# Sampling by ramps on row differences, with one four-bank spread tile, in a Trainium2 kernel

## The chip, the core and the metric

The kernel runs on one core of one Trainium2 chip. A core has a matrix engine (TensorE, in the profile PE, with its weight loads as PEld), a vector engine (VectorE, DVE), an activation engine (ScalarE, ACT), a general engine (GpSimd, POOL) and a queue engine (SyncE, SP) that here only issues DMA transfers. Matmuls write to PSUM, which is eight banks of 2 KB for each of 128 partitions; the other engines read it from there and work in SBUF. The engines run side by side, each through its own queue in order, and wait for one another through semaphores. The metric is the time of one execution of the whole kernel on the device, in microseconds (us). Lower is better.

## The reference

The network has four residual layers on an input of 16 images, 32 channels, 128 x 128. The change lies almost wholly in the second half of layer 1, a deformable convolution along y. For each image, each of K = 9 taps and each output place (r, c) an earlier stage gives a real row coordinate y. The tap k reads column c + k - 4 of the input at that row, by linear interpolation between two rows:

```
y0 = jnp.floor(gy)
...
w = (1.0 - jnp.abs(gx - xi)) * (1.0 - jnp.abs(gy - yi))
...
deformed = grid_sample_bilinear(input, grid)
out = conv2d(deformed, dsc_w, dsc_b, stride=(K, 1))
return group_norm(out, gn_w, gn_b, gn_w.shape[0] // 4)
```

The x coordinate is always whole, so only y is interpolated. The nine samples of a place are combined over channels and taps by the weights `dsc_w`; a group norm over groups of four channels follows, and the layer's input is added.

## The kernel before

The layers run one after another: `layer0`, `layer1_offsets`, `layer1_scan`, `layer1_sample`, `layer2`, `layer3_edges`, `layer3_net`. `layer1_sample` is the stage of the change. It has no gather. For one column c, the samples of all 128 places r are a matrix product: the image column as a 128 (rows) x 32 (channels) stationary operand, and a 128 x 128 matrix of hat functions, 1 - |y - row| where that is positive and 0 elsewhere, as the moving one. The stage builds those hats and multiplies.

An image is cut into 32 blocks of four columns; 16 images give 512 blocks. Block m is number n = m mod 32 of its image, and i = n mod 4 is its place in a group of four blocks, for which one convolution is done. For each block there are three kinds of hats:

- `ya`, taps 0 to 3, a 128 x 2048 tile. The y values lie as rows of the tile `Y`. Four matmuls (`spread`, L1212) copy one row of each tap onto all 128 partitions in PSUM, in tiles `pb` of two banks, of which there are two. ScalarE takes each half out as |y - row| (L1213), and VectorE makes the negative hat in place, min(t, 1) - 1 (`hats`, L1217).
- `yd`, taps 4 to 7, a 128 x 2048 tile. Here the DMA itself spreads: `fetch` (L1202) reads 8 KB of y and writes it to all 128 partitions, 1 MB for each block. ScalarE makes |y - row| in place (`absolutes`, L1333), VectorE the hat (L1217).
- `h8`, tap 8, once in four blocks (`eighth`), the same as `ya` from the tile `Y8`.

The sampling itself is `taps` (L1224): 16 matmuls for taps 0 to 3 and 16 for taps 4 to 7, each into a one-bank tile `pd` of which there are two; VectorE copies each to SBUF (`ds`, L1371 and L1377). `last_tap` does tap 8 for four blocks, and ScalarE copies it (L1398). `convolve` (L1259, L1264) multiplies a group's samples with the weights into `po`, ScalarE adds the bias (L1267). `turn` transposes the result through `pt` (L1276), VectorE copies it to `ob` (L1277). `finish` is the group norm of an image, given out in 22 small pieces, one at the end of each block, while the next image is sampled: eight pieces of statistics, two of sums over partitions, twelve of 128 x 1024 elementwise operations (L1320, L1322, L1324), of which each third adds the image `xt` as the residual and stores a quarter of the result.

The order on TensorE, VectorE and ScalarE is the order of the program: a helper, `in_order`, ties each instruction of these engines to the one before it. For block m the program writes: samples of `ya` of block m; `absolutes` and the hats `ya` of block m+1; copy; `near` (the spread of block m+2, with its two ScalarE operations); samples of `yd` of block m; hats `yd` of block m+1; copy. Then comes one of four extras: at i = 0 the convolution of the group before, at i = 1 its transposes, at i = 2 the spread for tap 8, at i = 3 the samples of tap 8. DMA issues on SP are not tied; the framework puts them where it expects their slot to be free. SP works through them in order, so a transfer whose slot is not yet free holds those behind it.

PSUM has eight banks: `pd` two, `po` and `pt` one each, `pb` four.

Of the kernel before, what the change touches and what calls it, by code (L numbers as in the profile page):

```python
# [10 lines left out]
F32 = mybir.dt.float32  # L11
AF = mybir.ActivationFunctionType
# [5 lines left out]
P = 128  # L18
# [50 lines left out]
def layer0(tc, w, x, x1, nb=B):  # L69
# [5 lines left out]
    with ExitStack() as ctx:  # L75
# [200 lines left out]
        def tail_z(st):  # L276
            b, t0 = st["b"], st["t0"]
            pz = ps_1.tile([P, 4, HW], F32, name="pz", tag="pz")
            for k in range(4):
                nc.tensor.matmul(pz[:, k], st["aT"][:, k], wadd, start=True, stop=False)  # L280
                nc.tensor.matmul(pz[:, k], st["mT"][:, k], wmod, start=False, stop=True)
            o = wp.tile([P, 4, HW], F32, name="o", tag="o")
            nc.vector.tensor_add(o, pz, xs[b][:, t0 : t0 + 4])
            r0 = (b % 4) * T + t0
            nc.sync.dma_start(x1[b // 4][r0 : r0 + 4].rearrange("t (c d) -> c t d", d=HW), o)

# [835 lines left out]
def layer1_sample(tc, w, x1, x2, ymap, sb1, batches=range(B)):  # L1122
# [8 lines left out]
    nc = tc.nc  # L1131
    V, S, M = nc.vector, nc.scalar, nc.tensor.matmul
    W4 = 4 * HW
    NB = HW // 4
    batches = list(batches)
    with ExitStack() as ctx:
        cp = ctx.enter_context(tc.tile_pool(name="cc", bufs=1))
        psd = ctx.enter_context(tc.tile_pool(name="cpd", bufs=2, space=PSUM))
        pso = ctx.enter_context(tc.tile_pool(name="cpo", bufs=1, space=PSUM))
        psb = ctx.enter_context(tc.tile_pool(name="cpb", bufs=2, space=PSUM))  # L1140
        dw4 = load(nc, cp, w["dsc_k4"], "dsc_k4")
# [3 lines left out]
        ident = load(nc, cp, w["ident"], "ident")  # L1145
        nrow = load(nc, cp, w["nrow"], "nrow")
        avg = cp.tile([P, P], F32, name="avg", tag="avg")
        V.memset(avg, 1.0 / P)

        sel = cp.tile([P, 32, P], F32, name="sel", tag="sel")  # L1150

        cb = cp.tile([P, NG, 4, 2], F32, name="cb", tag="cb")
        with tc.tile_pool(name="ct", bufs=1) as tp:
            e32 = load(nc, tp, w["eye32"], "eye32")
            V.tensor_copy(sel, e32.unsqueeze(2).to_broadcast([P, 32, P]))
            selq = load(nc, tp, w["selq"], "selq")
            for q in range(4):
                pq = psd.tile([P, NG, 2], F32, name="pq", tag="pd")
                M(pq, selq[:, q], sb1, start=True, stop=True)
                V.tensor_copy(cb[:, :, q], pq)  # L1160
            pb = pso.tile([P, NG, 4], F32, name="pbo", tag="po")
            for n, t in enumerate((dw4[:, 0], dw4[:, 1], dw8)):
                M(pb, t, cb[:, :, :, 1], start=(n == 0), stop=(n == 2))
            bos = cp.tile([P, NG, 4], F32, name="bos", tag="bos")
            V.tensor_scalar_add(bos, pb, bo)
# [12 lines left out]
        def open_image(b):  # L1178
            im = images[b] = {}
            g, j = divmod(b, 4)  # L1180
            im["Y"] = Y = yp.tile([P, W4], F32, name="Y", tag="Y")
            nc.sync.dma_start(Y, ym(b)[0:4].rearrange("k (n f) -> (k n) f", f=W4))
            im["Y8"] = Y8 = yp.tile([P, W4], F32, name="Y8", tag="Y8")
            y8 = ym(b)[8].rearrange("(s q f) -> q s f", q=4, f=W4)
            for q in range(4):
                nc.sync.dma_start(Y8[32 * q : 32 * q + 8], y8[q])
            im["xt"] = xt = xp.tile([P, T, HW], F32, name="xt", tag="xt")
            xg = x1[g][T * j : T * j + T].rearrange("o (r c) -> r o c", c=HW)
            for q in range(4):
                nc.sync.dma_start(xt[:, 8 * q : 8 * q + 8], xg[:, 8 * q : 8 * q + 8])  # L1190

            s = cb[:, g, j, 0:1]
            im["w4"] = w4 = sp.tile([P, 2, T], F32, name="w4", tag="w4")
            V.tensor_scalar(w4, dw4[:, :, 0:T], s, -1.0, ALU.mult, ALU.mult)
            im["w8"] = w8 = sp.tile([P, P], F32, name="w8", tag="w8")
            V.tensor_scalar(w8, dw8, s, -1.0, ALU.mult, ALU.mult)

        def fetch(m):
            b, n = order[m]
            blocks[m] = bl = {}  # L1200
            bl["yd"] = yd = hp.tile([P, 4, W4], F32, name="yd", tag="yd", bufs=4)
            nc.sync.dma_start(  # L1202
                yd, ym(b)[4:8, n * W4 : n * W4 + W4].unsqueeze(0).to_broadcast([P, 4, W4])
            )

        def spread(dst, Y, n, k):

            for h in range(2):
                pb = psb.tile([P, 2, W4], F32, name="pb", tag="pb")
                for a in range(2):  # L1210
                    q = 32 * (2 * h + a)
                    M(pb[:, a], sel[q : q + k, n], Y[q : q + k], start=True, stop=True)  # L1212
                S.activation(dst[:, 2 * h : 2 * h + 2], pb, AF.Abs, bias=nrow)  # L1213

        def hats(t):

            V.tensor_scalar(t, t, 1.0, 1.0, ALU.min, ALU.subtract)  # L1217

# [51 lines left out]
        def turn(b, s, oc):  # L1270

            if s == 0:
                images[b]["ob"] = xp.tile([P, T, HW], F32, name="ob", tag="ob")
            pt = pso.tile([P, 4, P], F32, name="pt", tag="pt")
            for i in range(4):
# [6 lines left out]
        def finish(b):  # L1282

            g, j = divmod(b, 4)
            im = images[b]
            ob, xt = im["ob"], im["xt"]
            st = sp.tile([P, 8, 6], F32, name="st", tag="st")
            mv = sp.tile([P, 8, 2], F32, name="mv", tag="mv")
            for og in range(8):
                V.bn_stats(st[:, og], ob[:, 4 * og : 4 * og + 4])  # L1290
                V.bn_aggr(mv[:, og], st[:, og])
                yield
            pm = pso.tile([P, 4, P], F32, name="pm", tag="pt")[:, 0, 0:8]
            M(pm, avg, mv[:, :, 0], start=True, stop=True)
# [6 lines left out]
            yield  # L1301
            pv = pso.tile([P, 4, P], F32, name="pv", tag="pt")[:, 0, 0:8]
            M(pv, avg, d, start=True, stop=True)
# [10 lines left out]
            for q in range(4):  # L1314
                o = slice(8 * q, 8 * q + 8)
                col = [
                    t.rearrange("p a b -> p (a b)")[:, o].unsqueeze(2).to_broadcast([P, 8, HW])
# [5 lines left out]
                yield  # L1323
                V.tensor_add(ob[:, o], ob[:, o], xt[:, o])  # L1324
                nc.gpsimd.dma_start(  # L1325
# [4 lines left out]

        def absolutes(m):
            yd = blocks[m]["yd"]
            S.activation(yd, yd, AF.Abs, bias=nrow)  # L1333

        def near(m):
            b, n = order[m]
            blocks[m]["ya"] = ya = hp.tile([P, 4, W4], F32, name="ya", tag="ya")
            spread(ya, images[b]["Y"], n, 32)

        def eighth(b, s):  # L1340
            h8 = hp.tile([P, 4, W4], F32, name="h8", tag="h8", bufs=2)
            spread(h8, images[b]["Y8"], s, 8)
            images[b]["h8", s] = h8

        open_image(batches[0])
        NM = len(order)
        for m in range(min(3, NM)):
            fetch(m)
        with in_order(tc, nc.tensor, nc.vector, nc.scalar):
            eighth(batches[0], 0)  # L1350
            near(0)
            absolutes(0)
            near(1)
            hats(images[batches[0]]["h8", 0])
            hats(blocks[0]["ya"])
            hats(blocks[0]["yd"])
            done = iter(())
            for m in range(NM + 6):
                b, n = order[m] if m < NM else (None, m - NM)
                if m < NM:  # L1360
                    bl = blocks[m]
                    bl["ds"] = dp.tile([P, 2, W4], F32, name="ds", tag="ds", bufs=6)
                    if n == 12 and m + NB < NM:
                        open_image(order[m + NB][0])
                    if m + 3 < NM:
                        fetch(m + 3)
                    pd = taps(m, 0, bl["ya"])
                    if m + 1 < NM:
                        absolutes(m + 1)
                        hats(blocks[m + 1]["ya"])  # L1370
                    V.tensor_copy(bl["ds"][:, 0], pd.rearrange("p i r -> p (i r)"))  # L1371
                    if m + 2 < NM:
                        near(m + 2)
                    pd = taps(m, 4, bl["yd"])
                    if m + 1 < NM:
                        hats(blocks[m + 1]["yd"])
                    V.tensor_copy(bl["ds"][:, 1], pd.rearrange("p i r -> p (i r)"))  # L1377
                s, i = divmod(n, 4)
# [16 lines left out]
                elif i == 3 and m < NM:  # L1395
# [4 lines left out]
                    if m + 1 < NM:  # L1400
                        nb_, nn = order[m + 1]
                        hats(images[nb_]["h8", nn // 4])
                next(done, None)
# [954 lines left out]
def network(ctx, tc, w, x, out):  # L2358
# [5 lines left out]

    x1 = [scratch([P, L], f"x1_{g}") for g in range(NG)]
    x2 = [scratch([P, L], f"x2_{g}") for g in range(NG)]
# [36 lines left out]
def pack(inp):  # L2403
# [104 lines left out]
    w["dsc_rows"] = np.tile(np.stack([i["gn_w"], i["gn_b"]])[None], (P, 1, 1))  # L2508
    w["nrow"] = -np.arange(P, dtype=f)[:, None]

# [96 lines left out]
```

## Time and profile before

| what | us |
|---|---|
| median of 3 runs | 16696.99 (16661.64 to 16734.23) |
| the profiled execution | 16668.54 |
| its span | 16666.3 |
| first sampling copy (L1371) to the last | 10778.7 to 13897.0 |
| TensorE busy over the span | 14464.2 |
| VectorE busy | 14412.7 |
| ScalarE busy | 12525.8 |
| GpSimd busy | 9711.4 |

A time in the profile is counted from the start of the span. A row of a group of instructions gives the line, the engine, the operation, what is written and read by the program's names, the shapes, the count, then the busy time in us with the mean of one instruction in ns, and last the idle time of the engine just ahead of them with what ended it. Neighbours on an engine overlap at their edges, so that sums of single durations come out some per cent above the engine's busy time. The clock column (PEclk) is the share of full speed that TensorE was granted; it is either 1 or 0.5 at any moment, so that its mean tells the share of time at half speed.

### The profile page before, as it was taken

To read this page: it belongs to the slowest core of one execution; us is meant where nothing else is said; L and a number is where in the kernel's file an instruction comes from. 1 tells how busy PE (TensorE), PEld (TensorE's weight loads), DVE (VectorE), ACT (ScalarE), POOL (GpSimd) and SP (SyncE) were. 2 spreads that over 40 slices of the span, in tenths; PEclk is the share of its full clock that TensorE was granted. 3 is DMA by queue.
4 is the path that set the end of the run, shared out by engine and by line. 5 is a ranking of instruction groups with operands and counts; after the bars stand their busy time and mean duration, and the time that the engine had idled before them with its cause. 6 is when DMAs were issued, how large, how long until landed. Compare 5 with 4: busy or idle time off the path is not lost. (4 is left out here: it accounts for less than half of the span.)

```text
span 16666.3 us, 327843 instructions
## 1 busy us (share of the span) xinstructions
PE 14464.2 (87%) x126810; PEld 5828.1 (35%) x126810; DVE 14412.7 (86%) x13784; ACT 12525.8 (75%) x25236; POOL 9711.4 (58%) x17789
## 2 busy tenths in 40 slices
PE   8998999989999888888888888899999997689966
PEld 3333333333333432222222222255555554434421
DVE  9999999999999659999999999888888886698622
ACT  8999999999999557777777777598888984466411
POOL 8999999999999457778887888500000001000012
PEclk9999999999999989999999999899899998789977
DMA  0000000000000334444454445578777876444356
GB/s 23 12 13 12 12 18 12 13 13 12 18 12 8 95 110 159 160 161 164 166 166 165 163 165 167 153 186 195 194 201 196 198 194 182 98 83 83 75 150 201
DMA packets 1347602, 1837.19 MB, mean 110 GB/s; under 512 B 161685, under 2 KB 661902, under 8 KB 1335799
## 3 DMA queue, kind: packets, MB, share of 16 engines
q1 hardware_dynamic: 1289910, 1655.23, 36.2%
q0 software_dynamic: 43840, 144.20, 2.4%
q8 instruction: 997, 16.33, 0.4%
q10 hardware_dynamic: 12288, 16.79, 0.4%
q14 instruction: 567, 4.64, 0.1%
HBM read 1497.44 MB, written 229.64 MB: 104 GB/s over the span
## 5 line engine op out<-in xcount | busy, mean ns | idle before, releaser
L235 POOL TENSOR_SCALAR Rp<-su,nv 128x128 f32<-128x128 f32 x15360 | 5406.6, 371 | 167.9 <-PE pS L241 133.0
L239 ACT ACTIVATE Ra<-su,bv 128x128 f32<-128x128 f32 x15360 | 4626.2, 390 | 406.7 <-PE pS L241 403.3
L224 DVE TENSOR_TENSOR Rd<-pu,nv 128x2048 f32<-128x2048 f32 x2176 | 4856.6, 2275 | 17.8 <-PE pS L241 16.8
L241 PE MATMUL pS<-Rd,zw 128*32 128x512 f32 x17408 | 2798.0, 606 | 378.7 <-DVE Rd L224 377.9
L919 DVE TENSOR_TENSOR_SCAN hh<-dd,state,pd 128x512 f32<-128x512 f32 x2304 | 2823.1, 1267 | 152.4 <-ACT ln L834 7.1
L940 POOL TENSOR_TENSOR hh<-hh,bc 128x2048 f32<-128x2048 f32 x512 | 2319.2, 4530 | 450.8 <-DVE state L927 439.8
L1325 POOL DMA_DIRECT2D x<-ob x64 | 92.0, 1438 | 3100.4 <-DVE ob L1324 2766.5
L904 PE MATMUL pd<-du,spread 32*128 32x512 f32 x4608 | 1340.1, 655 | 574.6 <-DVE hh L919 566.7
L896 ACT ACTIVATE dd<-dd,m_a 128x512 f32<-128x512 f32 x2304 | 1514.8, 713 | 335.3 <-DMA dd<-dm 328.9
L914 DVE TENSOR_TENSOR pd<-pd,bc 128x1024 f32<-128x1024 f32 x1152 | 1400.6, 1216 | 58.7 <-ACT bc L877 55.4
L241 PE MATMUL pS<-Rp,zw 128*32 128x512 f32 x7680 | 1314.3, 598 | 26.0 <-POOL Rp L235 25.9
L1333 ACT ACTIVATE yd<-yd,nrow 128x2048 f32<-128x2048 f32 x512 | 1238.1, 2418 | 56.7 <-DMA yd<-ymap 56.7
L1213 ACT ACTIVATE ya<-pb,nrow 128x1024 f32<-128x1024 f32 x1024 | 1196.7, 1260 | 80.6 <-PE pb L1212 80.1
L241 PE MATMUL pS<-Ra,zw 128*32 128x512 f32 x7680 | 1237.3, 601 | 0.0
L1212 PE MATMUL pb<-Y,sel 32*128 32x512 f32 (+1 forms) x5120 | 1075.3, 739 | 176.0 <-ACT ya L1213 172.8
L241 PEld LDWEIGHTS pS<-Rd,zw 128*32 128x32 f32 x17408 | 582.1, 109 | 1484.7 <-DVE Rd L224 927.4
L904 PEld LDWEIGHTS pd<-du,spread 32*128 32x128 f32 x4608 | 371.1, 189 | 1607.4 <-DVE hh L919 726.8
L1217 DVE TENSOR_SCALAR yd<-yd 128x2048 f32<-128x2048 f32 x512 | 727.5, 1421 | 207.0 <-ACT yd L1333 205.8
L1217 DVE TENSOR_SCALAR ya<-ya 128x2048 f32<-128x2048 f32 x512 | 759.0, 1482 | 10.7 <-ACT ya L1213 9.4
L1224 PE MATMUL pd<-ya,xt 128*32 128x128 f32 x16384 | 691.4, 311 | 42.5 <-DVE ds L1377 31.7
L1945 PE MATMUL ps<-t,W 128*128 128x512 f32 x1280 | 635.4, 644 | 80.9 <-DVE W L1925 53.1
L1224 PEld LDWEIGHTS pd<-yd,xt 128*32 128x32 f32 x16384 | 533.2, 178 | 471.0 <-issue 224.7
(434 smaller groups left out, 22927.2 us busy)
## 6 DMA issues: line engine op xcount, KB each, us to landing
dd<-dm SPq DMA_DIRECT2D x2304, 256.0 KB
yd<-ymap SPq DMA_DIRECT2D x512, 1024.0 KB
xq<-x SPq DMA_DIRECT2D x48, 1088.0 KB
dm<-dt POOLq DMA_DIRECT2D x192, 256.0 KB, 3.8
w<-d SPq DMA_DIRECT2D x512, 73.1 KB
xb<-tok SPq DMA_DIRECT2D x248, 144.0 KB
x<-in_x SPq DMA_DIRECT2D x64, 512.0 KB
x<-o SPq DMA_DIRECT2D x128, 256.0 KB
```

What stands on the lines that cost most here:

```text
L224: nc.vector.tensor_tensor(R, st["pu"].unsqueeze(1).to_broadcast([P, 4, 4, HW]), nv[:, :, i::32].rearrange("p t q -> p q t").unsqueeze(3).t ...
L235: nc.gpsimd.tensor_scalar(R[:, q, k], su[:, k], 3.4028234e38, nv[:, k, c], ALU.min, ALU.max)
L239: nc.scalar.activation(R[:, q, k], su[:, k], AF.Relu, bias=bv[:, k, c])
L241: nc.tensor.matmul(st["pS"][32 * q : 32 * q + 32], zw[:, 31 - i : 63 - i], R[:, q], start=first, stop=False, tile_position=(0, 32 * q), sk ...
L896: S.activation(dd[:, r], dd[:, r], AF.Exp, scale=acol[:, dr, d : d + 1])
L904: nc.tensor.matmul(pd[:, a], spread[e, k], st["du"][n][e], start=True, stop=True)
L914: V.tensor_mul(pd, pd, bm.unsqueeze(1).to_broadcast([P, 2, CH]))
L919: V.tensor_tensor_scan(hh[:, r, s], dd[:, r, s], pd[:, a, s], st["state"][:, 4 * i + r : 4 * i + r + 1], ALU.mult, ALU.add,)
L940: G.tensor_mul(hh, hh, st["bc"][1, n].unsqueeze(1).to_broadcast([P, 4, CH]))
L1217: V.tensor_scalar(t, t, 1.0, 1.0, ALU.min, ALU.subtract)
L1224: M(pd[32 * q : 32 * q + 32, i], xt[:, :, xc], h, start=True, stop=True, tile_position=(0, 32 * q),)
L1333: S.activation(yd, yd, AF.Abs, bias=nrow)
```

## The change

The interpolation is rewritten. With D[p] = x[p+1] - x[p], the sample at y is x[0] + sum over p of D[p] * clamp(y - p, 0, 1). The moving operand becomes a ramp, clamp(y - p, 0, 1), in place of a hat, and the stationary one the differences. Row 127 of the operand holds x[0] itself with a ramp that is always 1.

- `layer0` writes row 0 of each channel a second time behind the image (one more DMA of 2 KB for each output tile), and `x1` gets 128 more columns for it.
- `open_image` loads rows 1 to 128 into `xt`. `differ` loads rows 0 to 127 in quarters (`xq`) and GpSimd subtracts them, in blocks 24 to 27 of the image before. `finish` adds `xq`, loaded again by quarters, in place of `xt`. The y rows now lie in three tiles (`Y0`, `Y1`, `Y8`) with a row of ones beside each sixteen, loaded by 19 DMAs instead of 5; the ones and a 17th row of `sel` subtract the row number inside the spread matmul.
- `spread` writes all four matmuls into one `pb` tile of four banks, of which there is one. For `ya`, one VectorE operation takes it out, max 0 then min 1 (`ramp`), in place of two on ScalarE and one on VectorE. For `h8`, one ScalarE operation (Relu) and one VectorE clamp.
- `yd` is made by ScalarE in two halves (`ramps`, Relu with the bias -p), and clamped by VectorE (`clamps`).
- Both copies `ds` move from VectorE to ScalarE; `pd` has three banks instead of two. `pt` and `po` share one bank.
- `yd` has five buffers instead of four and is fetched four blocks ahead instead of three; ScalarE works on block m+2 of `yd` instead of m+1. GpSimd is tied to the program's order too.

```diff
-            nc.sync.dma_start(x1[b // 4][r0 : r0 + 4].rearrange("t (c d) -> c t d", d=HW), o)
+            nc.sync.dma_start(x1[b // 4][r0 : r0 + 4].rearrange("t (c d) -> c t d", d=HW)[0:P], o)
+            nc.sync.dma_start(x1[b // 4][r0 : r0 + 4, L:].unsqueeze(0), o[0:1])
...
-        psd = ctx.enter_context(tc.tile_pool(name="cpd", bufs=2, space=PSUM))
+        psd = ctx.enter_context(tc.tile_pool(name="cpd", bufs=3, space=PSUM))
         pso = ctx.enter_context(tc.tile_pool(name="cpo", bufs=1, space=PSUM))
-        psb = ctx.enter_context(tc.tile_pool(name="cpb", bufs=2, space=PSUM))
+        psb = ctx.enter_context(tc.tile_pool(name="cpb", bufs=1, space=PSUM))
...
+        def quarter(b, q):
+            g, j = divmod(b, 4)
+            xq = xp.tile([P, 8, HW], F32, name="xq", tag="xq")
+            xg = x1[g][T * j + 8 * q : T * j + 8 * q + 8].rearrange("o (r c) -> r o c", c=HW)
+            nc.sync.dma_start(xq, xg[0:P])
+            return xq
+
+        def differ(b, q):
+            xt = images[b]["xt"][0 : P - 1, 8 * q : 8 * q + 8]
+            G.tensor_sub(xt, xt, quarter(b, q)[0 : P - 1])
...
-        def spread(dst, Y, n, k):
-
-            for h in range(2):
-                pb = psb.tile([P, 2, W4], F32, name="pb", tag="pb")
-                for a in range(2):
-                    q = 32 * (2 * h + a)
-                    M(pb[:, a], sel[q : q + k, n], Y[q : q + k], start=True, stop=True)
-                S.activation(dst[:, 2 * h : 2 * h + 2], pb, AF.Abs, bias=nrow)
-
-        def hats(t):
-
-            V.tensor_scalar(t, t, 1.0, 1.0, ALU.min, ALU.subtract)
+        def spread(Y, n):
+
+            pb = psb.tile([P, 4, W4], F32, name="pb", tag="pb")
+            for a in range(4):
+                q = 32 * a
+                M(pb[:, a], sel[q : q + 17, n], Y[q : q + 17], start=True, stop=True)
+            return pb
+
+        def clamps(t):
+
+            V.tensor_scalar_min(t, t, 1.0)
...
+        def ramp(m):
             blocks[m]["ya"] = ya = hp.tile([P, 4, W4], F32, name="ya", tag="ya")
-            spread(ya, images[b]["Y"], n, 32)
+            V.tensor_scalar(ya, blocks[m].pop("pb"), 0.0, 1.0, ALU.max, ALU.min)
+
+        def ramps(m, h):
+            v = blocks[m]["yd"][:, 2 * h : 2 * h + 2]
+            S.activation(v, v, AF.Relu, bias=step)
 
         def eighth(b, s):
             h8 = hp.tile([P, 4, W4], F32, name="h8", tag="h8", bufs=2)
-            spread(h8, images[b]["Y8"], s, 8)
+            S.activation(h8, spread(images[b]["Y8"], s), AF.Relu)
             images[b]["h8", s] = h8
...
-                    if m + 3 < NM:
-                        fetch(m + 3)
-                    pd = taps(m, 0, bl["ya"])
-                    if m + 1 < NM:
-                        absolutes(m + 1)
-                        hats(blocks[m + 1]["ya"])
-                    V.tensor_copy(bl["ds"][:, 0], pd.rearrange("p i r -> p (i r)"))
+                    if 24 <= n < 28 and m + NB < NM:
+                        differ(order[m + NB][0], n - 24)
+                    if m + 4 < NM:
+                        fetch(m + 4)
+                    p0 = taps(m, 0, bl["ya"])
                     if m + 2 < NM:
                         near(m + 2)
-                    pd = taps(m, 4, bl["yd"])
+                    S.copy(bl["ds"][:, 0], p0.rearrange("p i r -> p (i r)"))
+                    if m + 2 < NM:
+                        ramp(m + 2)
+                        ramps(m + 2, 0)
+                    p4 = taps(m, 4, bl["yd"])
+                    S.copy(bl["ds"][:, 1], p4.rearrange("p i r -> p (i r)"))
+                    if m + 2 < NM:
+                        ramps(m + 2, 1)
                     if m + 1 < NM:
-                        hats(blocks[m + 1]["yd"])
-                    V.tensor_copy(bl["ds"][:, 1], pd.rearrange("p i r -> p (i r)"))
+                        clamps(blocks[m + 1]["yd"])
```

## The prediction

> **What bounds the kernel now.** I read the page's slices first (layer 1's sampling is the stretch from 10.74 to 13.9 ms), then the stage's own windows, its instruction groups, TensorE's order of time inside one group of four blocks, and last who waits for transfers. The first sampling copy starts at 10778.7 and the last at 13897.0: 3118.3 us for 511 steps, 6.10 us a block, 24.41 us a group of four. All that follows is counted in such groups, of which there are 128.
>
> The windows of the stage: stretch, its length, then busy time of PE, PEld, DVE, ACT and POOL, granted clock, DMA share, GB/s. The first is a long stretch, the other two are single groups.
>
> ```profile
> 11550.00:12340.00 790.00, 721.73 (x11246) 423.87 (x11240) 686.20 (x733) 702.63 (x519) 23.59 (x16) 0.91 0.80 195
> ...
> 12053.98:12078.24 24.26, 23.06 (x361) 13.25 (x355) 23.23 (x23) 21.37 (x17) 1.72 (x1) 0.86 0.82 199
> 12078.24:12101.71 23.47, 21.21 (x360) 12.49 (x354) 23.47 (x24) 22.60 (x18) 2.71 (x2) 1.00 0.89 232
> ```
>
> Three engines are at 87 to 91%, so no single one can be relieved for much. In the undisturbed group (clock 1.00) VectorE is busy throughout and ScalarE nearly so; the group with a spell at half clock is 0.8 us longer. Its neighbour before it, from 12029.19 to 12053.98, took 24.79 with such a spell too.
>
> The instruction groups that the change touches, and L224 of layer 0 as a row for its new operation:
>
> ```profile
> L224 DVE TENSOR_TENSOR Rd<-pu,nv 128x2048 f32<-128x2048 f32 x2176 | 4856.6, 2275 | 17.8 <-PE pS L241 16.8
> L1333 ACT ACTIVATE yd<-yd,nrow 128x2048 f32<-128x2048 f32 x512 | 1238.1, 2418 | 56.7 <-DMA yd<-ymap 56.7
> L1213 ACT ACTIVATE ya<-pb,nrow 128x1024 f32<-128x1024 f32 x1024 | 1196.7, 1260 | 80.6 <-PE pb L1212 80.1
> L1217 DVE TENSOR_SCALAR ya<-ya 128x2048 f32<-128x2048 f32 x512 | 759.0, 1482 | 10.7 <-ACT ya L1213 9.4
> L1217 DVE TENSOR_SCALAR yd<-yd 128x2048 f32<-128x2048 f32 x512 | 727.5, 1421 | 207.0 <-ACT yd L1333 205.8
> L1371 DVE COPY ds<-pd 128x512 f32<-128x512 f32 x512 | 374.3, 731 | 89.0 <-PE pd L1224 88.0
> L1398 ACT COPY ds<-pd 128x512 f32<-128x512 f32 x128 | 116.5, 910 | 32.9 <-PE pd L1224 32.4
> ```
>
> TensorE in order of time, from a block with i = 2 on:
>
> ```profile
> 12039.15 1.20 PE L1224 MATMUL pd<-yd,xt 128*32 128x128 f32 x32
> 12041.49 2.91 PE L1212 MATMUL pb<-Y,sel 8*128 8x512 f32 x8 [1.13 <-ACT ya L1213]
> 12044.33 2.06 PE L1224 MATMUL pd<-ya,xt 128*32 128x128 f32 x32
> 12046.32 2.09 PE L1212 MATMUL pb<-Y,sel 32*128 32x512 f32 x8
> 12048.34 1.67 PE L1224 MATMUL pd<-yd,xt 128*32 128x128 f32 x32
> 12049.82 1.07 PE L1224 MATMUL pd<-h,xt 128*32 128x128 f32 x32
> 12050.82 1.19 PE L1224 MATMUL pd<-ya,xt 128*32 128x128 f32 x32
> 12051.93 1.14 PE L1212 MATMUL pb<-Y,sel 32*128 32x512 f32 x8
> 12053.01 1.20 PE L1224 MATMUL pd<-yd,xt 128*32 128x128 f32 x32
> 12053.98 1.94 PE L1259 MATMUL po<-ds,w 128*32 128x512 f32 x16
> 12055.85 1.12 PE L1264 MATMUL po<-ds,w 128*128 128x512 f32 x2
> 12056.91 1.20 PE L1224 MATMUL pd<-ya,xt 128*32 128x128 f32 x32
> ```
>
> Start to start at full clock: samples of `ya` 1.11 us, a spread 1.08, samples of `yd` about 1.0, convolution 2.93, samples of tap 8 1.0; the transposes are 0.66. The spread for tap 8 stood 1.13 us for a `pb` tile that ScalarE still held, and after that gap the next bursts took 2.06 and 2.09 in place of 1.2 and 1.14: the matrix engine lost its clock for some 8 us. With a mean clock of 0.91, 18% of the time is at half speed, 4.4 us a group, so about 0.55 such spells a group; one costs now about 1.0 us (24.26 and 24.79 against 23.47).
>
> The waits of the stage for transfers:
>
> ```profile
> ACT yd L1333 <- DMA yd<-ymap: 56.7, 14, 6.8
> ```
>
> Fourteen times in all `yd` was late, 56.7/128 = 0.44 us a group. So 23.47 + 0.55 + 0.44 = 24.46 is the 24.41 measured.
>
> **What the change moves, in sums a group.** ScalarE loses eight `ya` halves (8 x 1.26) and two of tap 8 (2.5), gains eight copies (8 x 0.58 to 0.91; the low end is the 128x512 copy of L877 at 582 ns) and one 128x2048 Relu (2.42 by L1333); four `yd` operations become eight halves (4 x 2.42 to 8 x 1.26). From 24.1 to between 18.4 and 21.6. VectorE loses four hats (4 x 1.48) and eight copies (5.9), gains four ramps. A ramp is new: 128x2048 out of PSUM in one operation. The low end is L224, 2.275, which reads as much from PSUM; the high end four copies `ds`, 4 x 0.731 = 2.92, with four starts. I take 2.5, near the first since it is one instruction, but with the sampling burst always beside it (a `yd` hat is 1.184 at its fastest, 1.421 in the mean). VectorE goes from 23.4 to about 21.6. TensorE's work is the same. By sums alone the change wins about 1.8 us a group.
>
> The row says that PSUM costs VectorE double: a hat of 2048 from SBUF takes 1.184 at best, a copy of 512 from PSUM 0.616. [...]
>
> **What stands on the path.** The sums do not decide, because there is now one `pb`. Each spread must wait until the tile of the one before is read out as a whole. I follow one group at full clock, handoffs at 0.05 (the chain shows 0.03 to 0.04). VectorE's `finish` pieces are 8 x (0.80 + 0.20) + 12 x 1.45 + 1.7 = 27.1 an image, 0.85 a block. Zero is the start of the spread in the block with i = 1.
> - i = 1: spread to 1.08; ramp 1.13 to 3.63, clamp (1.42) to 5.05, copy `ob` (0.70) to 5.75, piece to 6.60. TensorE: samples, transposes, samples, then the next spread 3.85 to 4.93, samples to 5.93.
> - i = 2: VectorE reaches this ramp at 6.60, ends 9.10. Only then may tap 8's spread start: 9.15 to 10.23, TensorE idle 3.2. ScalarE reads it out 10.28 to 12.70. TensorE does one sampling to 11.34 and waits again, 1.4, for the tile; the next spread is 12.75 to 13.83. VectorE had ended clamp and piece at 11.37 and stands 2.5.
> - i = 3: ramp to 16.38, clamp, tap 8's clamp (1.71), piece to 20.36. TensorE: two samplings and tap 8's, next spread 16.94 to 18.02.
> - i = 0: samples, convolution, samples to 23.06; the ramp is over at 22.86. The next spread starts at 23.06.
>
> So 23.1 at full clock against 23.47: what is taken off the engines comes back as waits for the one tile. With a ramp of 2.275 it is 22.6, with 2.92 about 24.2.
>
> The gap of 3.2 us ahead of tap 8's spread is three times the one that cost the clock in about half of the groups. I take 0.75 spells a group, between the 0.55 of now and 1. A spell here lies on the path: tap 8's spread +1.0, the next spread +1.0, the sampling after it +0.5, as the rows at 12041 to 12048 show; 2.5 in all. 0.75 x 2.5 = 1.9. [...]
>
> Late `yd`: now the four loads of `xt` wait for the last residual add and go in a row. After, `xt` is free earlier, but eight quarters an image more (0.5 MB each) pass the same SP queue, some of which wait for GpSimd's subtraction, with `yd` fetches behind them and ScalarE behind those. Between 0 and 8 us an image (twice the 3.70 that ScalarE stood at 12110 for four such loads), 0 to 1.0 a group; I take 0.3, a little under the present 0.44. GpSimd's 64 subtractions (2.34 each by the 128x1024 row of layer 1's scan) have four blocks to spare.
>
> Sum a group: 23.06 + 1.9 + 0.3 = 25.27, against 24.41: +0.86 x 128 = +110 us.
>
> **Ahead of the loop.** From the first load of the stage (10731.1) to the first sampling (10770.1) it is 39 us now. Two images' y loads are issued before the rest, 28 issues more at 0.43 = 12 us; and the first samples need all four quarters of differences, two rounds of a load (about 5) and a subtraction (2.34), 15 us. +27, bounds +10 and +45. I take +30 with the two operand tables.
>
> Layer 0's extra 128 issues (0.36 each on SP, 2 KB) stand beside a stage where GpSimd, ScalarE and VectorE are the busy ones and SP is idle: 0; if a queue were held by each, 46 us. Rows of `x1` now 512 bytes longer: 0, no row says otherwise.
>
> Total: 16668.5 + 110 + 30 = 16809; the median is 28 above that execution, so about 16840.
>
> **Rivals.** *It gets faster* (0.23). The ramp is near 2.275 and the clock is lost no more often or dearly than now: 22.6 + 0.55 + 0.1 = 23.25, -1.16 x 128 + 30 = -118, about 16580. For it: all engines' sums fall, and full clock often outlasts a gap. Against it: the wait for tap 8's bank is in the order itself. It decides as soon as spells cost less than 0.8 us a group. *The transfers become the bound* (0.12): ScalarE, two blocks ahead, stands 8 us an image more: 16840 + 130 = 16970. For it: DMA share 0.80 and 4 MB more an image; against it: slices at over 340 GB/s show room. *The gains and waits cancel* (0.15): 0.55 spells of 2.5 and `yd` as now, 23.06 + 1.4 + 0.1 = 24.5, with the start +40: 16735. The forecast has 0.50.
>
> **How the numbers follow.** About 0.5% (83 us) is what a measurement of this kernel tells from none. Most of the first rival lies below 16613, some between; the third lies in the band, with the forecast's low edge. Faster 0.20, same 0.25, slower 0.55. The forecast's own range (spells 0.55 to 1, ramp 2.275 to 2.7) is 16740 to 16960; with the rivals 16590 to 17030.
>
> **What would show it.** Right: in the group of tap 8's spread TensorE idle 2.5 to 3.5 us for VectorE's ramp, then 1 to 1.5 for ScalarE's h8; half clock in more than 18% of the stage; ramps of 2.3 to 2.7 us; ScalarE under 85% busy. Wrong: these gaps under 1 us each, a clock over 0.93, or a ramp near 1.5; or `yd` waits of over 100 us, which would make it slower than I say.

## The result and the profile after

The changed kernel takes 16931.64 us in the median (16916.57 to 16976.81, 4 runs), beside 16689.22 us (16661.64 to 16734.23, 4 runs) for the kernel before in the same series. The ratio is 1.0147, 95% interval 1.0117 to 1.0177: about 1.5% slower. The forecast was 16840, so it had the sign, and was 92 us short.

The profiled execution took 16935.22 us, against 16668.54. Where the 266.7 us between them lie, by the first or last instruction of each stage:

| part | before | after | difference |
|---|---|---|---|
| start to the last instruction of layer 0 | 5584.1 | 5586.7 | +2.6 |
| from there to the last scan operation of layer 1 (offsets, scan, set-up) | 5137.9 | 5188.9 | +51.0 |
| last scan operation to the first sampling copy | 56.7 | 76.4 | +19.7 |
| first sampling copy to the last (the loop) | 3118.3 | 3316.7 | +198.4 |
| all after it | 2769.3 | 2764.5 | -4.8 |

The code of the offsets and of the scan is not touched. Over the profiles of this study the scan alone took from 4651 to 4775 us (before 4664, after 4709), so that most of the 51 us there is the spread between executions. The offsets read `x1`, whose rows are longer now: in the nine profiles with longer rows they end 3 to 10 us later behind layer 0 than in the profile before, which the prediction put at nothing. What the change costs is the loop and its start, 218 us; by the medians it is 242.

The window of the loop after (stretch, length, busy time of PE, PEld, DVE, ACT and POOL, granted clock, DMA share, GB/s):

```profile
10900.00:14150.00 3250.00, 2825.25 (x43818) 1748.51 (x43818) 2482.14 (x1835) 2282.78 (x2397) 225.13 (x116) 0.83 0.78 204
```

VectorE was at 87% in the stretch shown of before and is at 76%, ScalarE fell from 89% to 70%, just as the change says. Yet the loop is longer, and the clock fell from 0.91 to 0.83: TensorE now spends 34% of the loop at half speed, before 18%. A group of four blocks takes 25.96 us in place of 24.41.

The groups of instructions in the loop (busy and mean of one, then the idle time before them and its releasers):

```profile
L1362 DVE TENSOR_SCALAR ya<-pb 128x2048 f32<-128x2048 f32 x512 | 1267.6, 2476 | 744.2 <-PE pb L1236 742.9
L1236 PE MATMUL pb<-Y,sel 17*128 17x512 f32 x5120 | 912.5, 780 | 379.4 <-DVE ya L1362 263.5 <-ACT h L1370 102.0 <-DMA Y<-ymap 6.3
L1366 ACT ACTIVATE yd<-yd,step 128x1024 f32<-128x1024 f32 x1024 | 1434.7, 1401 | 116.7 <-DMA yd<-ymap 115.0 <-DVE ob L1301 1.0 <-DVE yd L1241 0.7
L1241 DVE TENSOR_SCALAR yd<-yd 128x2048 f32<-128x2048 f32 x512 | 709.3, 1385 | 1.2 <-ACT yd L1366 1.2
L1406 ACT COPY ds<-pd 128x512 f32<-128x512 f32 x512 | 311.8, 609 | 168.4 <-PE pd L1248 163.7 <-ACT h L1370 0.3
L1370 ACT ACTIVATE h<-pb 128x2048 f32<-128x2048 f32 x128 | 256.7, 2005 | 277.1 <-PE pb L1236 277.1
```

The ramp takes 2.476 us. It and its spread wait for each other: VectorE stood 742.9 us for `pb` to be filled, TensorE 263.5 us for VectorE to empty it and 102.0 for ScalarE. Before, TensorE stood 167.1 us for `pb` in the same stretch. The third wait is the one for `yd`, 115.0 us against 56.7.

One block with i = 2 and the next, from the timeline of the profile after (start, length, engine and line):

```profile
12032.13 1.19 PE L1248 MATMUL pd<-yd,xt 128*32 128x128 f32 x32
...
12033.70 2.30 DVE L1362 TENSOR_SCALAR ya<-pb 128x2048 f32<-128x2048 f32 x1
12036.06 1.14 PE L1236 MATMUL pb<-Y,sel 17*128 17x512 f32 x8 [2.73 <-DVE ya L1362]
12037.13 1.98 PE L1248 MATMUL pd<-ya,xt 128*32 128x128 f32 x32
12037.27 2.07 ACT L1370 ACTIVATE h<-pb 128x2048 f32<-128x2048 f32 x1 [2.24 <-PE pb L1236]
...
12039.39 2.09 PE L1236 MATMUL pb<-Y,sel 17*128 17x512 f32 x8 [0.28 <-ACT h L1370]
...
12041.41 2.00 PE L1248 MATMUL pd<-yd,xt 128*32 128x128 f32 x32
12041.55 2.32 DVE L1362 TENSOR_SCALAR ya<-pb 128x2048 f32<-128x2048 f32 x1 [2.95 <-PE pb L1236]
12043.16 1.63 PE L1248 MATMUL pd<-h,xt 128*32 128x128 f32 x32
...
12044.60 1.13 PE L1248 MATMUL pd<-ya,xt 128*32 128x128 f32 x32
```

This is the walk of the prediction. Tap 8's spread stands 2.73 us for the ramp; then the bursts take 1.98, 2.09, 2.00 and 1.63 us until the clock is back at 12044.60; the second wait, for ScalarE's `h`, is 0.28 here because the slow burst fills the gap (about 1.05 us in the 16 groups where the burst between ran at full clock); VectorE stands 2.95 us for the spread behind it.

The same stretch shows the transfers, 20 us later:

```profile
12038.62 15.21 SPq L1216 DMA_DIRECT2D xq<-x  x4
...
12053.92 1.80 SPq L1227 DMA_DIRECT2D yd<-ymap  x1
...
12063.17 1.15 ACT L1366 ACTIVATE yd<-yd,step 128x1024 f32<-128x1024 f32 x1 [6.57 <-DMA yd<-ymap]
...
12067.66 2.09 PE L1236 MATMUL pb<-Y,sel 17*128 17x512 f32 x8 [4.43 <-ACT h L1370]
```

SP held four issues of `xq` for 15.2 us, one of `yd` stood behind them, ScalarE stood 6.57 us for its data, and as `h` comes after that on ScalarE, TensorE stood 4.43 us for `pb`.

By place in the image, groups counted from convolution to convolution, in us:

| blocks | 0-3 | 4-7 | 8-11 | 12-15 | 16-19 | 20-23 | 24-27 | 28-31 |
|---|---|---|---|---|---|---|---|---|
| before | 23.9 | 23.7 | 25.3 | 24.0 | 23.9 | 23.6 | 26.9 | 23.8 |
| after | 25.5 | 25.9 | 28.8 | 25.2 | 26.0 | 25.2 | 27.5 | 23.3 |

Two places stand out. At 24-27 are the differences and their loads. At 8-11 is something that the prediction does not have: `finish` writes its means `pm` into the bank of `pt`, at the end of the very block that transposes into `pt`. From the timeline of after:

```profile
11325.95 0.74 DVE L1301 COPY ob<-pt 128x512 f32<-128x512 f32 x1
...
11326.74 0.39 PE L1318 MATMUL pm<-mv,avg 128*128 128x8 f32 x2 [2.60 <-DVE ob L1301]
```

TensorE stands 2.60 us, in the middle of its queue, until VectorE comes to the copy of `pt`, which is behind a ramp and a clamp. The wait itself is not new, since `pm` lay in the bank of `pt` in the kernel before too; it got longer. The waits of the stage before and after (us in total, times, longest):

```profile
PE pm L1294 <- DVE ob L1277: 25.8, 15, 2.0
```
```profile
PE pm L1318 <- DVE ob L1301: 38.5, 15, 2.7
```

That is 1.7 us an image before and 2.6 after. Beside its two neighbours the group at 8-11 was 1.5 us longer before and is 3.2 us longer now.

### The profile page after: what moved, and what is told of

The parts are those of the page before. It is cut to its first block, busy times and chain, and to the rows that moved or that the text cites. A ratio compares the mean times of both kernels' runs of the same rounds, so it can differ in the third digit from the quotient of the medians.

```text
span 16933.2 us, 329420 instructions
## 1 busy us (share of the span) xinstructions
PE 14527.3 (86%) x126810; PEld 5941.3 (35%) x126810; DVE 14225.6 (84%) x12761; ACT 12054.3 (71%) x25620; POOL 9866.1 (58%) x17853
## 4 chain that ended last, share of the span: by engine, by line
DVE 36%; PE 35%; ACT 11%; issue 8%; POOL 4%; DMA 3%; SPq 3%; DVEq 0%; ACTq 0%; POOLq 0%
DVE hh L920 12%; DVE Rd L224 8%; PE pS L241 7%; ACT Ra L239 6%; DVE pd L915 5%; PE pd L1248 5%; PE ps L1983 4%; PE pb L1236 4%; PE ps L512 4%; POOL Rp L235 3%; DVE ya L1362 2%; PE pd L905 1%; ACT h L1370 1%; PE po L1283 1%; SPq L2331 1%
## 5 line engine op out<-in xcount | busy, mean ns | idle before, releaser
L224 DVE TENSOR_TENSOR Rd<-pu,nv 128x2048 f32<-128x2048 f32 x2176 | 4857.9, 2277 | 19.8 <-PE pS L241 18.7
L1362 DVE TENSOR_SCALAR ya<-pb 128x2048 f32<-128x2048 f32 x512 | 1267.6, 2476 | 744.2 <-PE pb L1236 742.9
L1350 POOL DMA_DIRECT2D x<-ob x64 | 57.8, 903 | 3029.5 <-DVE ob L1349 3011.6
L1366 ACT ACTIVATE yd<-yd,step 128x1024 f32<-128x1024 f32 x1024 | 1434.7, 1401 | 116.7 <-DMA yd<-ymap 115.0
L241 PE MATMUL pS<-Rp,zw 128*32 128x512 f32 x7680 | 1308.5, 596 | 25.3 <-POOL Rp L235 25.3
L1236 PE MATMUL pb<-Y,sel 17*128 17x512 f32 x5120 | 912.5, 780 | 379.4 <-DVE ya L1362 263.5
L1248 PEld LDWEIGHTS pd<-yd,xt 128*32 128x32 f32 x16384 | 588.7, 179 | 512.3 <-ACT ds L1406 267.3
L1248 PE MATMUL pd<-yd,xt 128*32 128x128 f32 x16384 | 731.4, 325 | 21.4 <-DVE yd L1241 9.4
L1248 PE MATMUL pd<-ya,xt 128*32 128x128 f32 x16384 | 726.6, 324 | 21.3 <-POOL xt L1221 17.8
```

The costliest lines, as they stand in the source:

```text
L224: nc.vector.tensor_tensor(R, st["pu"].unsqueeze(1).to_broadcast([P, 4, 4, HW]), nv[:, :, i::32].rearrange("p t q -> p q t").unsqueeze(3).t ...
L241: nc.tensor.matmul(st["pS"][32 * q : 32 * q + 32], zw[:, 31 - i : 63 - i], R[:, q], start=first, stop=False, tile_position=(0, 32 * q), sk ...
L1236: M(pb[:, a], sel[q : q + 17, n], Y[q : q + 17], start=True, stop=True)
L1248: M(pd[32 * q : 32 * q + 32, i], xt[:, :, xc], h, start=True, stop=True, tile_position=(0, 32 * q),)
L1362: V.tensor_scalar(ya, blocks[m].pop("pb"), 0.0, 1.0, ALU.max, ALU.min)
```

## The experiments

The theory: one `pb` tile for both uses, with tap 8's spread between two ramps, makes the wait, and the clock and the late transfers add to it. The rivals: the lost clock itself is most of it; the transfers are; the one large operation is. For one expectation below, that the bank shared with `po` makes `pm` wait, the rows above already say that the wait is older than the change. Total times go by their ratio to the kernel before; the 1.0147 of the changed kernel has itself an interval of 0.003 to each side, some 50 us. "Share with a spell" is the part of the groups in which over a tenth of the sampling matmuls took over 0.4 us (0.64 before, 0.91 after).

**Tap 8 out of the one tile.** Each of the four matmuls of its spread goes into a sample bank, one in each block, and ScalarE takes it out by quarters. VectorE's clamp of it moves from the block with i = 3 to the next one with i = 0:

```diff
+        def eighth_part(b, s, a):
...
+            pd = psd.tile([P, 4, HW], F32, name="pd", tag="pd").rearrange("p i r -> p (i r)")
+            q = 32 * a
+            M(pd, sel[q : q + 17, s], images[b]["Y8"][q : q + 17], start=True, stop=True)
+            S.activation(images[b]["h8", s][:, a], pd, AF.Relu)
...
-                elif i == 2 and m + 2 < NM:
-                    nb_, nn = order[m + 2]
-                    eighth(nb_, nn // 4)
```

> Tap 8's spread leaves the four-bank tile: one of its four matmuls in each block, each into a one-bank sample tile, read out by ScalarE in four operations of 128x512 in place of one of 128x2048. Theory of the one tile (tap 8's spread waits for the ramp before it, and the next spread waits for tap 8's Relu, on TensorE's own queue): both waits go, the group falls from 25.96 us to between 22.3 and 23.3, the kernel from 16932 to between 16460 and 16590, below the kernel before. Theory of the transfers (the loop is longer because y arrives late behind the extra loads of x): VectorE's and ScalarE's order hardly matters, the time stays within 50 us of 16932, and the waits of ScalarE for yd stay near 115 us.

16774.29 us (10 runs), ratio 1.0032, 1.0014 to 1.0049. The loop is 3127 us, 189 shorter; the clock in it:

```profile
10980.00:14040.00 3060.00, 2914.17 (x43805) 1643.48 (x43800) 2583.84 (x1836) 2406.49 (x2767) 223.54 (x116) 0.95 0.85 216
```

TensorE's wait for VectorE at `pb` falls from 263.5 to 34.2 us, the share with a spell from 0.91 to 0.20, the median group from 25.14 to 23.27. The theory holds, and this is the largest single part of the loss: the ratio falls by 1.15 points, some 190 us. But the time expected was lower by 184 us and more: the ordinary groups are where they were expected, and those at 8-11 (28.6), 24-27 (25.2) and 0-3 (25.3) are not. So the rest lies in those places.

**The clock alone.** The order stays; TensorE gets unused matmuls ahead of the two spreads, so that it is not idle in the gaps:

```diff
+        def busy(t, times):
+            pd = psd.tile([P, 4, HW], F32, name="pd", tag="pd").rearrange("p i r -> p (i r)")
+            for _ in range(times):
+                M(pd, avg, t[:, 0], start=True, stop=True)
...
+                    if n % 4 == 3:
+                        busy(bl["yd"], 1)
...
+                    if n % 4 == 2:
+                        busy(bl["yd"], 2)
```

> The order stays; in the block with i = 2 TensorE does two matmuls of 128x128 by 128x512 (1.07 us each) into an unused sample tile ahead of tap 8's spread, and in the block with i = 3 one ahead of the next spread: the idle time is filled with work that nobody reads. Theory of the clock (most of the loss is that these gaps cost TensorE half its clock for some 7 us in 9 of 10 groups): spells fall to 0.3 a group or less, the granted clock in the stage rises from 0.86 to 0.93 or more, and the time falls by some 1.2 to 1.8 us a group, to between 16700 and 16780. Theory of the waits alone (the clock only shows the idle time): the waits stand as before, the time stays within 40 us of 16932, or rises where the filling work ends after the wait.

16858.08 us (16847.11 to 17032.61, 4 runs), ratio 1.0108, 1.0055 to 1.0160. The loop of the profiled execution is 3256 us, 61 shorter, and the ratio falls by 0.39 points, 65 us. (That execution is the longest of the four; layer 0, which ends 92 us later than in the changed kernel, and the scan, 66 us longer, are untouched code.) The clock is back:

```profile
11060.00:14200.00 3140.00, 2841.51 (x43924) 1635.63 (x43928) 2480.59 (x1812) 2256.20 (x2361) 221.35 (x114) 0.96 0.82 207
```

The share with a spell is 0.28, and the time at half clock in the loop falls from 1133 to 290 us by the clock records of the traces (with tap 8 in the sample banks it is 314). So with nearly the clock of the run above, the loop is still 129 us longer than there: the waits are there without the spells, and the clock alone is not the cause. The fillers cost something themselves. In the groups of the first image without a spell, where no `finish` runs, the mean is 22.95 here (6 groups, median 22.5) and 22.15 after (4 groups, median 21.9); some 0.6 us a group is an estimate of it, from few groups. Without it the spells' price would be some 140 us rather than 61.

**The differences left out.**

```diff
-        for q in range(4):
-            differ(batches[0], q)
...
-                    if 24 <= n < 28 and m + NB < NM:
-                        differ(order[m + NB][0], n - 24)
```

> Left out: the differences of rows (the 64 loads of quarters for them and GpSimd's 64 subtractions), so that the samples are of rows and not of differences. Theory of the transfers: ScalarE's waits for yd fall from 115 us to 40 or less, the start of the loop comes some 20 us earlier, and the time falls by 100 us or more, to 16830 or below. Theory of the one tile with the clock: only these two direct terms go, the groups outside of n = 24 to 27 stay at 25 to 26 us, and the time falls by 60 to 120 us. Above 16890 the extra loads would cost next to nothing.

16866.00 us, ratio 1.0094, 1.0069 to 1.0119; the loop 3244 us, 72 shorter, and the start 63 us in place of 76. The ratio falls by 0.53 points, 88 us: inside the 60 to 120 of the second theory, short of the 100 or more of the first. By place only one changes much, 24-27, from 27.5 to 24.0. ScalarE's wait for transfers:

```profile
ACT yd L1366 <- DMA yd<-ymap: 19.1, 8, 6.8
```

It was 115.0. So the loads and subtractions of the differences together are worth 72 us of the loop and 13 of its start.

**Two tiles of two banks, the ramp in halves.** The same four banks, handed over by twos:

```diff
-        psb = ctx.enter_context(tc.tile_pool(name="cpb", bufs=1, space=PSUM))
+        psb = ctx.enter_context(tc.tile_pool(name="cpb", bufs=2, space=PSUM))
...
+            for h, pb in enumerate(blocks[m].pop("pb")):
+                V.tensor_scalar(ya[:, 2 * h : 2 * h + 2], pb, 0.0, 1.0, ALU.max, ALU.min)
```

> The spread tile goes back to two tiles of two banks: the ramp is two VectorE operations of 128x1024 and tap 8's Relu two of ScalarE. Theory of the one tile: a half is free 1.2 us earlier, tap 8's spread and the one after it each start earlier, the path of a group is 1 to 2 us shorter and the gap ahead of tap 8's spread falls from 2.7 to 1.5 us or less: the time falls to between 16650 and 16800. Theory that one VectorE operation of four banks saves more than it holds up: two starts more a block (some 0.1 us each) make it slower, 16940 to 17000.

16894.42 us, ratio 1.0110, 1.0087 to 1.0134; the loop 3279 us, 38 shorter, the share with a spell 0.88. The expectation of a larger gain fell. TensorE's wait for VectorE at `pb` goes from 263.5 to 122.9 us, but that for ScalarE is still 50.7, and the clock stays at 0.84. In the median of 127 groups the gap ahead of tap 8's spread falls from 2.3 to 1.2 us, as expected, but the spread itself then takes 2.4 us in place of 1.4: with tap 8 behind the ramp, an earlier first half moves the wait rather than closing it. Against the 189 us of the run that took tap 8 out, the size of the operation is the smaller part.

**The mean one block later.**

```diff
                 V.bn_aggr(mv[:, og], st[:, og])
                 yield
+            yield
             pm = pso.tile([P, 4, P], F32, name="pm", tag="po")[:, 0, 0:8]
```

> The changed kernel with one edit: in finish the first sum over partitions (pm) comes one block later, after the block of the transposes instead of in it, and the 13 pieces behind it a block later too. Seen in the changed kernel: pm, which shares its bank with the transposes now, stands 2.6 us for VectorE's copy of them, right ahead of the samplings, and the group there (n = 8 to 11) takes 28.8 us against 25 to 26 elsewhere (25.3 in the kernel before). Theory of the shared bank: this group falls to 26 or less, 3 us or more an image, 40 to 60 us in all, to 16870 to 16890. Rival (that group is long because it has the most small VectorE work, wherever the sum stands): no change within 20 us.

16881.88 us, ratio 1.0107, 1.0086 to 1.0129: 0.40 points, 67 us, below the changed kernel's, though the two intervals overlap. The groups at 8-11 fall from 28.8 to 24.1, and the wait of `pm` for `ob` is gone from the list, so it is the place of `pm` and not the small VectorE work that makes them long. What the same edit is worth in the kernel before, where `pm` stands too, was not tried. The loop gains only 34 us of the 75 that this is worth over 16 images: the groups at 28-31 rise from 23.3 to 28.6, and ScalarE's waits for `yd` from 115.0 to 163.4 us. `finish` now ends one block later, closer to the differences, which use the same `xq` tiles. That this nearness is the cause was not tried by itself.

**Both.** Tap 8 in the sample banks and the late mean together:

> Tap 8 through the sample banks, and the sum over partitions one block later. Theory: the group n = 8 to 11, 28.6 us with tap 8 in the sample banks, falls to 24.5 or less, since the clock is not lost there either; 4 us an image or more, 65 us or more in all, 16774 to 16690 to 16710. Rival: as with the sum moved alone, no change within 20 us.

16637.38 us (16593.26 to 16678.93, 5 runs), ratio 0.9952, 0.9932 to 0.9972: faster than before, and better than expected. The loop is 3049 us, 268 shorter than the changed kernel's, where the two alone gave 189 and 34. The groups are 22.8, 22.7, 23.0, 23.0, 23.1, 26.1, 23.6 and 25.6 from 4-7 on: only 24-27 and 0-3 stand out, and it is from 24 on into the next image's first group that ScalarE waits for `yd`, 158.4 us in all.

**The quarters on GpSimd's queue.** The run before, and in `quarter`:

```diff
-            nc.sync.dma_start(xq, xg[0:P])
+            nc.gpsimd.dma_start(xq, xg[0:P])
```

> As the kernel with both edits, and the 128 quarter loads of xq are issued by GpSimd's queue instead of SP's, so that no fetch of yd stands behind a load that waits for GpSimd's subtraction. Theory (the cost of the transfers is their place in SP's queue): the waits of ScalarE for yd fall to under 60 us, the group n = 24 to 27 falls from 25 us to 23.5, and the time by 30 to 60 us more, to 16640 to 16680, about the time of the kernel before or under it. Rival (the transfers cost by their share of the DMA engines): the waits for yd stay over 90 us and the time within 20 us of the kernel with both edits. Third: GpSimd's queue, tied to the program's order, brings quarters too late for VectorE's residual add, and it is slower.

16734.44 us (10 runs), ratio 1.0009, 0.9996 to 1.0021: a loss of 0.57 points against the run before. It is a miss, and the waits say why:

```profile
POOL xt L1221 <- DMA xq<-x: 374.9, 47, 12.1
PEld pd L1248 <- POOL xt L1221: 164.4, 15, 25.5
```

The waits for `yd` fell from 158.4 to 2.2 us, so the fetches had stood behind `xq` on SP's queue. But the first samples of an image now stood for the differences, 15 times, 164.4 us; the group at 28-31 took 32.8. GpSimd's queue in order of time:

```profile
12602.27 4.37 POOL L1221 TENSOR_TENSOR xt<-xt,xq 127x1024 f32<-127x1024 f32 x1 [14.55 <-PE pd L1248]
12606.55 0.90 POOL L1216 DMA_DIRECT2D xq<-x  x1
12617.81 2.85 POOL L1221 TENSOR_TENSOR xt<-xt,xq 127x1024 f32<-127x1024 f32 x1 [10.36 <-DMA xq<-x]
12620.58 1.76 POOL L1216 DMA_DIRECT2D xq<-x  x1
12630.25 2.33 POOL L1221 TENSOR_TENSOR xt<-xt,xq 127x1024 f32<-127x1024 f32 x1 [7.92 <-DMA xq<-x]
```

In program order a quarter is issued after the subtraction of the one before, so that load and subtraction alternate, 12 to 16 us a quarter in these rows, where a block takes 6.

**The quarters issued one step ahead.**

```diff
-            G.tensor_sub(xt, xt, quarter(b, q)[0 : P - 1])
+            xq = ahead.pop((b, q)) if (b, q) in ahead else quarter(b, q)
+            if q < 3:
+                ahead[b, q + 1] = quarter(b, q + 1)
+            G.tensor_sub(xt, xt, xq[0 : P - 1])
...
+                    if n == 23 and m + NB < NM:
+                        ahead[order[m + NB][0], 0] = quarter(order[m + NB][0], 0)
```

> The kernel with tap 8 in the sample banks, the late mean and the quarters of the differences on GpSimd's own queue; each quarter is now issued one step ahead of the subtraction that needs the one before it. In the run without this, GpSimd issued a load only after the subtraction before it, so that one step took 10 to 13 us where a block takes 6, and the first samples of an image stood 164.4 us in all for the differences (15 times); ScalarE's waits for yd had gone from 158.4 to 2.2 us. Theory that the issue order on GpSimd was what took the gain back: both waits are now small, the group that starts an image falls from 32.8 to about 24, the group comes to 23.2 and the time to 16540 to 16600. Rival, that the loads themselves take 10 us and more because the DMA engines are full: the wait for the differences stays over 80 us, and the time stays at 16640 or above.

16572.30 us (16546.50 to 16650.25, 7 runs) beside 16684.47 (12 runs), ratio 0.9934, 0.9910 to 0.9958: the lowest ratio of all, in the range expected, though its interval overlaps that of the run with both edits (0.9932 to 0.9972). The loop is 2980 us, 69 shorter than in that run, a group 23.33, the one at 28-31 22.4.

```profile
10860.00:13780.00 2920.00, 2836.56 (x43927) 1609.54 (x43919) 2621.23 (x1838) 2445.06 (x2774) 356.88 (x232) 0.98 0.85 226
```
```profile
POOL xt L1224 <- DMA xq<-x: 167.6, 32, 8.4
PEld pd L1251 <- POOL xt L1224: 26.2, 1, 26.2
...
ACT yd L1370 <- DMA yd<-ymap: 7.1, 8, 1.6
```

Both waits are small at once (the 26.2 us are the start of the loop). TensorE is busy 97% of the loop at a clock of 0.98. The DMA engines are as busy as in the run before (a share of 0.85, there 0.86 over the loop): so what the run before lost was lost by the order on the queues.

## Why the prediction was right, and where it was off

*The sign and its mechanism* were right. VectorE and ScalarE lost work, and what the sums gave (1.8 us a group) came back as the waits for the one tile. Taking tap 8 out of it is worth 189 us of the loop and leaves median groups at 23.27. The size was short: +143 us was forecast (+110 for the loop, +30 for the start), +242 came by the medians, +198 for the loop.

*The ramp* at 2.5 us measured 2.476: the row of L224 was the right neighbour. That PSUM costs VectorE double, as the prediction read from its rows, comes out at 1.8 times here: 2.476 us from PSUM, beside 1.385 for the clamp of as many values in SBUF. *The gap* ahead of tap 8's spread was put at 3.2 and is 2.3 us in the median, the next one at 1.4 and is about 1.05 where the clock stays up (`h` took 2.005, not 2.42); VectorE's stand of 2.5 is 3.5 in the median. ScalarE is at 70%, under the 85% named. *Layer 0* was put at 0 and shows +2.6. *The start* was put at +30 and is +20.

*The group at full clock*, 23.06, can't be read from the changed kernel, where only 11 of 127 groups are undisturbed, 4 of them in the first image (mean 21.8). With the fillers, the 85 undisturbed groups behind the first image have a mean of 23.9; less the 0.6 estimated for the fillers, 23.3. The term stands within what that can tell.

*The spells*, 0.75 x 2.5 = 1.9 us a group. The time at half speed is 8.9 us a group, twice the 4.4 of before, but not by their number. The clock records of the traces hold 107 stretches at half clock in the loop before, 5.2 us each in the mean (0.84 a group), and 117 of 9.7 us after (0.92). The prediction had 0.55 and 0.75 of one length, 8 us; what grew is the length. Their price looks too high: with the fillers the loop lost 61 us net, 0.5 us a group, or 1.1 with the estimate for the fillers. A reason may be that the second gap is partly filled by the slow bursts, as the 0.28 us above shows for one group. How many of the 2.5 us a single spell costs is not settled closer than that.

*Late `yd`*, 0.3 a group: this term failed in size. The wait is 115.0 us, 0.9 a group, near its upper bound of 1.0, and leaving the differences out shortens the loop by 72 us, 0.57 a group, with 19.1 us of such waits still left. The mechanism was named (`xq` ahead of `yd` on SP's queue); it was "four blocks to spare" for the subtractions that made it look cheap. They have the time; the fetches queued behind their loads have not.

*What the walk left out* is `pm`. It has VectorE's copy of `pt` end at 5.75, some 3 us behind the transposes, but has nothing on TensorE wait for that copy; the trace has `pm` stand 2.6 us there, once an image. It is not the bank shared with `po` that makes it stand, since it stood 1.7 us in the kernel before; the ramp and the clamp ahead of the copy made the wait longer. The change's own share is some 1.8 us an image (3.2 less 1.5 above the neighbours), an estimate of 27 us in all; the 75 us that the later mean takes off this place hold what was there before as well.

The loop was 88 us longer than forecast, 0.69 a group. Late `yd` above its 0.3 is 0.27 a group by the run without differences and 0.6 by the wait, 35 to 77 us, and `pm` some 27. That is about the size of the miss, but the spells' true price is not known, so the runs do not divide it further.

Some sums of the prediction are slightly off: the group adds up to 25.26, not 25.27; ScalarE's low end is 18.6, not 18.4; with a ramp of 2.92 the walk gives 24.6, not 24.2; the third rival comes to some 16750, not 16735. None of them moves the forecast.

*The rivals.* "It gets faster" was to decide when spells cost less than 0.8 us a group; the net 0.5 of the fillers is under that and 1.1 with their own cost taken out is not, so the runs do not test this condition cleanly. "The transfers become the bound" was half right: 72 us, not 130.

## What to carry to other kernels

A tile that two consumers on different engines take turns at is a chain of its own (here tap 8's turn at it cost 189 us of the loop): follow it around the loop before counting what the engines save, and when two tiles are merged into one, or a bank has two uses, list each writer and what its reader is queued behind. An issue queue in order is such a chain too: a load that has time to spare still holds the ones behind it (here four of `xq` held SP for 15.2 us, and ScalarE stood 6.57 us for the `yd` behind them), and on an engine that also computes, a load has to be issued ahead of the work that waits for the one before (on GpSimd's queue the samples' wait for the differences fell by that from 164.4 to 26.2 us). A change that is slower as made may hold its gain: with two waits and one queue put right, this one came out 0.66% faster than the kernel before. One of these edits, the later mean, could be made in the kernel before as well, so not all of the 0.66% need be the change's.

## What the runs showed of the hardware

TensorE's clock went after gaps of little over 1 us, and mostly more often after longer ones. Gaps between TensorE's instructions in the loop, counted as followed by a spell if over 30% of the sampling matmuls in the next 4 us took over 0.4 us: before, 48% of 101 gaps of 1.0 to 1.3 us and all of 12 of 3.6 to 6.0; after, 68% of 34 gaps of 1.3 to 1.6, 92% of 85 gaps of 2 to 3, all of 12 above 3. It is not the gap alone: 18 gaps of 1.0 to 1.3 us in the changed kernel were followed by one in 22%, 7 gaps of 1.3 to 1.6 in the kernel before by none, and 29 such gaps in the run with two tiles of two banks in 97%. What else decides was not tried.

ScalarE's copies of 128x512 from PSUM were put at 0.58 to 0.91 us; moved behind the sampling bursts they took 0.609 and 0.653 in the mean (L1406 and L1411), where tap 8's, beside a burst, had taken 0.910 before. The traces show the same within one line of the changed kernel: of L1411's copies at full clock, the 98 wholly beside a burst of `ya` samples took 0.93 us in the median, the 242 with no sampling matmul beside them 0.585. At half clock the 111 beside a burst of `h` took 0.587. What it is in the burst that slows them is not shown.
